# Sharing the adds of an attention layer between TensorE and VectorE: one gathered chunk of four on TensorE, or two

## The chip, the cores and the metric

The kernel runs as one program on one core of a Trainium2 chip. The metric is the device time of one execution in microseconds (us), from the first to the last instruction. Three executions of the kernel before took 1926.28, 1930.35 and 1936.67 us; their median, 1930.35 us, is the time before. About half a per cent (some 10 us) is what a measurement of this kernel can tell from no change: the three runs lie 0.5% apart.

The engines are named as in the profile: PE is TensorE (matmuls; PEld is its weight loads), DVE is VectorE, ACT is ScalarE, POOL is GpSimd, SP is the engine that issues most plain DMAs. "Granted clock" is the share of its full clock that TensorE is allowed at a time.

## The reference

The program is a graph network of four layers on 2708 nodes with 128 features, each followed by a residual add and a layer norm. Only the last layer, layer 3, is touched. For each of four heads it computes, with x the nodes' features and A the (sparse) adjacency matrix,

```
x1 = x @ w1
x2 = x @ w2
E  = leaky_relu(x1[:, None, :] + x2[None, :, :], negative_slope=0.01)
s  = E @ a
s  = tanh(s / 8.0) * 8.0
s  = exp(s) * A
s  = s / sum(s, axis=-1)
out = leaky_relu(s @ x @ Wlin.T, negative_slope=0.01)
```

and then joins the heads with one more matrix `w`. So every edge (i, j) needs, for each head, 128 sums x1[i] + x2[j], a leaky relu of each, and the dot product of the result with the head's vector `a`. The kernel writes leaky_relu(z) as 0.01 z + 0.99 max(z, 0). The first part is linear and is kept as four ready numbers per node; what is left per edge is max(z, 0) times 0.99 a, summed over 128 features, for four heads: 512 products and four sums.

## The kernel before, in words

The adjacency matrix has about 0.6% of its entries set, so the kernel lists each node's edges and works on edges. Nodes are sorted by degree and laid out in 24 blocks (`BLOCKS3`, lines 47 to 51). A block is cut into *steps* (`quads`, line 1527): 100 in all; fifteen of the 24 blocks have four or five. One step handles four *chunks*, and a chunk is up to 128 edges, one edge to a partition.

For a step `i` the loop at line 1541 does this:

- POOL gathers, one indirect DMA per chunk (`fetch`, line 1530; `gather`, line 246), one row per edge from a table in DRAM: 512 numbers of x2 (four heads of 128), 128 of x, and four linear terms. The row lands in `g4[:, r, :]`, r from 0 to 3. Nine such buffers (`GOT`) stand ready, so POOL runs up to eight steps ahead.
- PE puts x1 of each edge's own node into PSUM (`repeated`, line 1350): for chunk r a matmul whose weights are rows 32r to 32r+31 of a table of zeros and ones, so the four chunks use four different strips of the array. Chunks 0 to 2 go to three banks of the tile `z3`, chunk 3 to the tile `z1`. A further matmul, with the 128x128 identity as weights, adds chunk 3's gathered x2 onto `z1` (line 1363). Both tiles have one buffer, so the matmuls for step i+1 wait until step i has been read.
- DVE adds `z3` to the gathered x2 of chunks 0 to 2 (line 1555), in place in `g4`. Then it finishes chunk 3 with four instructions, one per head, that take max(z, 0) * 0.99a and the sum over 128 features at once (`scores`, line 1373). Then the products of the other chunks (`products`, line 1381), in place: three chunks in an even step (56 of the 100), two in an odd step (44).
- ACT sums the products, one instruction per chunk and head, with the sum falling out beside a dummy output (`sums_of_products`, line 1389): 12 in an even step, 8 in an odd one. In an odd step DVE does chunk 2 with four more instructions of line 1373.

Between these, `step()` (line 1514) lets three queues of unfinished work advance by one piece each, three times in a loop pass: `closing` (`rest`, line 1394: after each pair of steps, the linear terms, tanh and exp, the softmax sum by a small matmul at line 1414, its reciprocal at 1419, the weights `wm` at 1422, and eight matmuls at line 1435 that weigh and add the gathered x); `finishing` (`finish`, line 1443: once per block, a copy of that result, matmuls with Wlin at 1456, leaky relu by 1461 on ACT and 1463 on DVE, matmuls with w at 1469 and 1475); and `preparing` (`own_terms`, line 1311: x1 of the next block by the matmuls 1316, 1323 and 1324, the copies 1319 and 1327 on ACT, and line 1330 on DVE).

The program holds the order of each of PE, DVE and ACT as it is written (`manual_schedule`, line 1249); each works its list strictly in that order. On PE, the matmuls of `repeated` for step i+1 stand behind the first `step()` of step i and ahead of its products.

Of the kernel before, what the change touches and what calls it, by code (L numbers as in the profile page):

```python
# [9 lines left out]
FP = mybir.dt.float32  # L10
AF = mybir.ActivationFunctionType
ALU = mybir.AluOpType
# [3 lines left out]
P = 128  # L16
# [13 lines left out]
HD = HEADS * D  # L30
# [55 lines left out]
def gnn_resnorm_kernel(  # L86
# [21 lines left out]
    nc = tc.nc  # L108

    const = ctx.enter_context(tc.tile_pool(name="const", bufs=1))  # L110
    ident = const.tile([P, P], FP, name="ident")
# [225 lines left out]
    with ExitStack() as layer:  # L337
# [316 lines left out]
        for g in KINDS:  # L654
            j = 32 // g
# [198 lines left out]
        def own_row(b):  # L854
            n = BLOCKS[b][1]
            x_s = mine.tile([P, 2, D], FP, name="x_s", bufs=3)
            nc.sync.dma_start(
                x_s[0:n],
                dx_dram[int(b >= SPLIT)][b * P : b * P + n, 0 : 2 * D].rearrange(
                    "p (t d) -> p t d", t=2  # L860
                ),
            )
            return x_s
# [169 lines left out]
        ahead = own_row(0)  # L1033
        left = list(range(SPLIT, NBLK))
        for i, b in enumerate(TURNS):
            if i == SPLIT - 2:
                sorted_lists(1)
            x_s, ahead = ahead, own_row(TURNS[i + 1]) if i + 1 < NBLK else None
# [7 lines left out]
            for _ in range(2 if i < 1 else 1):  # L1046
                if left:
                    e = left.pop(0)
# [15 lines left out]
            for _ in range(2 if i in (9, 10, 11) else 1):  # L1064
                if i and again:
                    e = again.pop(0)
# [31 lines left out]
    with ExitStack() as layer:  # L1098
# [26 lines left out]
        for b0, count, n in quads():  # L1125
            a = accs2[b0 // 4].rearrange("p (j d) -> p j d", d=D)[0:n, b0 % 4 : b0 % 4 + count]
            h = hb[0:n, b0 : b0 + count]
# [3 lines left out]
            for j in range(count):  # L1131
                nc.tensor.matmul(
                    ps_v[:, 0:D], lhsT=ones[0:n, :], rhs=sq[0:n, j, :],
                    start=(b0 + j == 0), stop=(b0 + j == NBLK - 1),
# [48 lines left out]
        for b0, count, n in quads():  # L1183
            h = hb[0:n, b0 : b0 + count]
# [54 lines left out]
    with ExitStack() as layer:  # L1239
# [4 lines left out]
        ps_z = layer.enter_context(tc.tile_pool(name="s3_ps_z", bufs=1, space=PSUM))  # L1244
# [18 lines left out]
        a_99 = work.tile([P, HEADS, D], FP, name="a_99")  # L1263
        nc.vector.tensor_scalar(a_99, a_all, 0.99, None, ALU.mult)
        a_ps = ps_a.tile([P, HD], FP, name="a_ps")
# [84 lines left out]
        def repeated(b, j, g4):  # L1350

            g, _ = BLOCKS3[b]
            e = g * (P // g)
            z3 = ps_z.tile([P, 3, HD], FP, name="z3")
            z1 = ps_z.tile([P, HD], FP, name="z1")
            for r in range(4):
                rows = slice(32 * r, 32 * r + 32)
                nc.tensor.matmul(  # L1358
                    z3[0:e, r, :] if r < 3 else z1[0:e],
                    lhsT=copies[g][rows, j, :], rhs=own[b][1][rows, :],  # L1360
                    start=True, stop=r < 3, skip_group_check=r == 3,
                )
            nc.tensor.matmul(  # L1363
                z1[0:e], lhsT=ident[0:e, 0:e], rhs=g4[0:e, 3, 0:HD],
                start=False, stop=True, skip_group_check=True,
            )
            return z3, z1

        def scores(e, r, z, a, g4, sc):

            for hd in range(HEADS):
                part_of = slice(hd * D, (hd + 1) * D)
                nc.vector.scalar_tensor_tensor(  # L1373
                    g4[0:e, r, part_of], z[0:e, part_of], 0.0, a[0:e, part_of],
                    ALU.max, ALU.mult, accum_out=sc[0:e, hd : hd + 1],
                )

        def products(e, g4, count):

            z = g4[0:e, 0:count, 0:HD]  # L1380
            nc.vector.scalar_tensor_tensor(  # L1381
                z, z, 0.0, a_ps[0:e].unsqueeze(1).to_broadcast((e, count, HD)), ALU.max, ALU.mult
            )

        def sums_of_products(e, g4, sc, count):
            for r in range(count):
                for hd in range(HEADS):
                    junk = small.tile([P, D], BF, name="sum_junk")
                    nc.scalar.activation(  # L1389
                        junk[0:e], g4[0:e, r, hd * D : (hd + 1) * D], AF.Identity,  # L1390
                        accum_out=sc[0:e, r, hd : hd + 1],
                    )
# [121 lines left out]
        def step(early=True):  # L1514
            for queue, most in ((finishing, 1), (closing, 2), (preparing, 1)):
                if queue is not preparing or early:
                    for work_of in list(queue[:most]):
                        if next(work_of, "done") == "done":
                            queue.remove(work_of)

        def prepare(b):
            own[b] = (own_rows(b),)
            yield from own_terms(b)
# [4 lines left out]
        gathered = {}  # L1528

        def fetch(i):  # L1530
            b, j = quads[i]
            e = BLOCKS3[b][0] * (P // BLOCKS3[b][0])
            g4 = got.tile([P, 4, RW], FP, name="g4")
            for r in range(4):
                ch = CHUNK3[b] + 4 * j + r
                gather(g4[0:e, r, :], t2_dram, idx3[0:e, ch : ch + 1])
            gathered[i] = g4

        fetch(0)
        ahead = repeated(*quads[0], gathered[0])  # L1540
        for i, (b, j) in enumerate(quads):
            g, jj = BLOCKS3[b]
            e = g * (P // g)
            if j == 0:
                if b + 1 < NB3:
                    preparing.append(prepare(b + 1))
            if j % 2 == 0:
                sc, g4s = small.tile([P, 8, HEADS], FP, name="sc_s", bufs=4), []
            g4, (z3, z1) = gathered.pop(i), ahead
            g4s.append(g4)  # L1550
            sc4 = sc[:, 4 * (j % 2) : 4 * (j % 2) + 4, :]
            if i + 1 < len(quads):
                fetch(i + 1)
            z = g4[0:e, 0:3, 0:HD]
            nc.vector.tensor_tensor(z, z, z3[0:e], ALU.add)  # L1555
            scores(e, 3, z1, a_99.rearrange("p h d -> p (h d)"), g4, sc4[:, 3, :])
            step()
            if i + 1 < len(quads):
                while quads[i + 1][0] not in own or len(own[quads[i + 1][0]]) < 3:
                    step()  # L1560
                ahead = repeated(*quads[i + 1], gathered[i + 1])
            count = 2 if j % 2 else 3
            products(e, g4, count)
            step()
            sums_of_products(e, g4, sc4, count)
            if count == 2:
                scores(e, 2, g4[:, 2, 0:HD], a_ps, g4, sc4[:, 2, :])
            step()
            if j % 2 or j == jj - 1:
                closing.append(rest(b, list(range(j - j % 2, j + 1)), g4s, sc))  # L1570
# [526 lines left out]
```

## Time and profile before

| what | value |
|---|---|
| median of three runs | 1930.35 us |
| profiled execution, its own time | 1936.67 us |
| its span, first to last instruction | 1936.7 us |
| layer 3's loop, from the first matmul of line 1358 to the last gathered step's work | 1122 to 1905 us, 783 us |
| PE busy, share of the whole span, granted clock | 64%, 0.667 of full |
| DVE, ACT, POOL busy, share of the whole span | 60%, 40%, 46% |

The profiled execution is the slowest of the three, 0.3% above the median, and its span is the whole of its time. Shares over the whole span average four layers with different limits; what matters here is the loop of layer 3, two fifths of the time. The chain of waits that the page gives ends in the output's write and does not reach back into the loop, so the loop has to be read from its waits, groups, timeline and windows.

### The profile page before, as it was taken

The numbers are of one execution on the slowest core, as the hardware profiler recorded it, in microseconds if no ns is written. First come the engines' busy times: TensorE is split into PE (matmuls) and PEld (weight loads), VectorE is DVE, ScalarE is ACT, GpSimd is POOL, SyncE is SP. The second block draws the span as 40 slices with busy tenths as digits, with TensorE's granted clock in tenths as the row PEclk, the third lists the DMA queues.
The fourth block names the chain that finished last, engine by engine and source line by source line (L and its number), as shares of the span: only waits on it lengthen the run. The fifth ranks groups of instructions, "written<-read, shape, count | busy, mean of one in ns | idle before, by whom it ended". The sixth has DMA issues, their size and how long they took to land. (4 is left out here: it accounts for less than half of the span.)

```text
span 1936.7 us, 23643 instructions
## 1 busy us (share of the span) xinstructions
PE 1240.9 (64%) x5771; PEld 864.1 (45%) x5771; DVE 1166.6 (60%) x4895; ACT 776.5 (40%) x3156; POOL 892.8 (46%) x1003
## 2 busy tenths in 40 slices
PE   7974313353446553554673748888788788878885
PEld 7973212242334442554663314544444444444444
DVE  8997445675635423433447417777678677676774
ACT  3565345543324210211122415555455555445553
POOL 1004654445653366445331474655555556555430
PEclk9986555555555576776676756676676777666675
DMA  8642645666545525223231574865566655756540
GB/s 283 238 150 79 131 140 165 174 183 174 141 103 142 177 43 160 95 92 140 79 113 44 167 239 131 212 190 163 145 196 183 182 166 160 191 150 192 150 115 7
DMA packets 167676, 289.63 MB, mean 150 GB/s; under 512 B 49600, under 2 KB 121502, under 8 KB 160429
## 3 DMA queue, kind: packets, MB, share of 16 engines
q0 software_dynamic: 60496, 190.77, 34.4%
q1 hardware_dynamic: 99489, 92.57, 15.6%
q10 hardware_dynamic: 7544, 4.69, 1.0%
q8 instruction: 48, 0.79, 0.2%
q14 instruction: 99, 0.81, 0.1%
HBM read 242.51 MB, written 45.36 MB: 149 GB/s over the span
## 5 line engine op out<-in xcount | busy, mean ns | idle before, releaser
L247 POOL DMA_INDIRECT g<-t_dram,idx x400 | 398.6, 996 | 316.0 <-issue 178.9
L247 POOL DMA_INDIRECT msg<-d_dram,idx x368 | 348.6, 947 | 260.2 <-issue 164.8
L1389 ACT ACTIVATE sum_junk<-g 126x128 bf16<-126x128 f32 (+3 forms) x1024 | 301.3, 296 | 142.4 <-issue 59.8
L1358 PE MATMUL z<-x,copies 32*126 32x512 f32 (+3 forms) x800 | 221.3, 944 | 65.8 <-DVE g L1555 45.0
L969 PE MATMUL pt_a<-ident,rows 128*128 128x128 f32 (+2 forms) x475 | 114.1, 395 | 144.4 <-ACT at_sb L974 79.5
L1555 DVE TENSOR_TENSOR g<-g,z 126x1536 f32<-126x1536 f32 (+3 forms) x100 | 175.0, 1750 | 44.0 <-DMA g<-t_dram,idx 15.3
L1018 PE MATMUL acc<-x_nat,at_rows 128*128 128x128 f32 (+2 forms) x968 | 160.7, 326 | 52.3 <-DMA at_rows<-at_dram,perm 26.5
L1389 ACT ACTIVATION_READ_ACCUMULATOR sum_junk<-g 126x1 f32 (+3 forms) x1024 | 191.6, 187 | 0.0
L1018 PEld LDWEIGHTS acc<-x_nat,at_rows 128*128 128x128 f32 (+2 forms) x968 | 144.1, 232 | 65.5 <-issue 38.7
L1363 PE MATMUL z<-g,ident 126*126 126x512 f32 (+3 forms) x200 | 169.3, 941 | 0.7 <-issue 0.7
L1435 PE MATMUL po_s<-wm,g 126*128 126x24 f32 (+6 forms) x800 | 128.6, 316 | 58.5 <-DVE wm L1422 56.2
L1435 PEld LDWEIGHTS po_s<-wm,g 126*128 126x128 f32 (+3 forms) x800 | 124.8, 243 | 75.6 <-DVE wm L1422 67.9
L969 PEld LDWEIGHTS pt_a<-ident,rows 128*128 128x128 f32 (+2 forms) x475 | 82.9, 205 | 167.5 <-ACT at_sb L974 92.8
L884 DVE SCALAR_TENSOR_TENSOR own<-msg,ls,own 128x128 f32<-128x128 f32 (+1 forms) x302 | 105.6, 350 | 85.4 <-ACT msg L899 28.5
L1381 DVE SCALAR_TENSOR_TENSOR g<-g,a_ps 126x1536 f32<-126x1536 f32 (+6 forms) x100 | 151.0, 1510 | 0.0
L420 PE MATMUL acc<-x_nat,rows 128*128 128x129 f32 (+3 forms) x1012 | 128.5, 288 | 26.0 <-DMA rows<-in_adj_dram 14.9
L420 PEld LDWEIGHTS acc<-x_nat,rows 128*128 128x128 f32 (+2 forms) x1012 | 123.0, 198 | 31.2 <-DMA rows<-in_adj_dram 16.0
L1358 PEld LDWEIGHTS z<-x,copies 32*126 32x126 f32 (+3 forms) x800 | 67.8, 261 | 100.3 <-issue 46.5
L899 ACT ACTIVATE msg<-msg 128x896 f32<-128x896 f32 (+4 forms) x55 | 50.4, 917 | 132.9 <-DVE msg L896 92.1
L1373 DVE SCALAR_TENSOR_TENSOR g<-z,a 126x128 f32<-126x128 f32 (+3 forms) x400 | 91.9, 285 | 19.5 <-remote 9.2
L445 DVE FIND_INDEX8 ci<-cv,rows 128x8 uint32<-128x247 f32 (+2 forms) x242 | 98.7, 408 | 0.0
L1363 PEld LDWEIGHTS z<-g,ident 126*126 126x126 f32 (+3 forms) x200 | 42.0, 263 | 124.3 <-issue 117.3
(302 smaller groups left out, 2132.2 us busy)
## 6 DMA issues: line engine op xcount, KB each, us to landing
rows<-in_adj_dram SPq DMA_DIRECT2D x34, 1354.0 KB
at_dram<-at_sb SPq DMA_DIRECT2D x105, 256.0 KB
g<-t_dram,idx POOLq DMA_INDIRECT x400
msg<-d_dram,idx POOLq DMA_INDIRECT x368
t_dram<-t_row SPq DMA_DIRECT2D x21, 256.0 KB
x_s<-dx_dram SPq DMA_DIRECT2D x21, 128.0 KB
at_dram<-at_sb SPq DMA_DIRECT2D x21, 64.0 KB
t_dram<-x_nat SPq DMA_DIRECT2D x5, 256.0 KB
```

The costliest lines, as they stand in the source:

```text
L247: nc.gpsimd.indirect_dma_start(out=dst, out_offset=None, in_=table[0:N, :], in_offset=bass.IndirectOffsetOnAxis(ap=index, axis=0),)
L420: nc.tensor.matmul(accs0[k][0:m, c0 : c0 + f1 - f0], lhsT=rows[0:n, j0 : j0 + m], rhs=x_nat[0:n, b, f0:f1], start=k not in started, stop=( ...
L445: nc.vector.max_index(out=ci[0:n, at], in_max=cv[0:n, at], in_values=rows[0:n, c0 : c0 + cw])
L884: nc.vector.scalar_tensor_tensor(to, m, v, last, ALU.mult, ALU.add)
L969: nc.tensor.transpose(pt[0:m, j, 0:n], rows[0:n, c0 : c0 + m], ident[0:n, 0:n])
L1018: nc.tensor.matmul(accs2[ib // 4][0:m, (ib % 4) * D : (ib % 4 + 1) * D], lhsT=at[0:n, i0 : i0 + m], rhs=xw[0:n, b, :], start=(k == 0 and i ...
L1358: nc.tensor.matmul(z3[0:e, r, :] if r < 3 else z1[0:e], lhsT=copies[g][rows, j, :], rhs=own[b][1][rows, :], start=True, stop=r < 3, skip_g ...
L1363: nc.tensor.matmul(z1[0:e], lhsT=ident[0:e, 0:e], rhs=g4[0:e, 3, 0:HD], start=False, stop=True, skip_group_check=True,)
L1381: nc.vector.scalar_tensor_tensor(z, z, 0.0, a_ps[0:e].unsqueeze(1).to_broadcast((e, count, HD)), ALU.max, ALU.mult)
L1389: nc.scalar.activation(junk[0:e], g4[0:e, r, hd * D : (hd + 1) * D], AF.Identity, accum_out=sc[0:e, r, hd : hd + 1],)
L1435: nc.tensor.matmul(po[:, p0 * HEADS : (p0 + g) * HEADS], lhsT=g4s[i][0:e, r, HD : HD + D], rhs=wm[0:e, 4 * i + r, :, :], start=True, stop= ...
L1555: nc.vector.tensor_tensor(z, z, z3[0:e], ALU.add)
```

## The change

`repeated` now leaves x1 of chunks 0 and 1 in a two-bank tile `z2` and gives chunks 2 and 3 a tile of one bank each (`z1_2`, `z1_3`, together `zs`); it adds the gathered x2 to both by the identity. PSUM use stays at four banks. DVE adds only chunks 0 and 1. Chunk 2's products become one DVE instruction that reads `zs[0]` in PSUM and writes over the gathered x2. `products` always handles two chunks. ACT sums chunks 2, 0 and 1, in that order, in every step, and DVE's four extra instructions in odd steps are gone.

```diff
-            z3 = ps_z.tile([P, 3, HD], FP, name="z3")
-            z1 = ps_z.tile([P, HD], FP, name="z1")
+            z2 = ps_z.tile([P, 2, HD], FP, name="z2")
+            zs = [ps_z.tile([P, HD], FP, name=f"z1_{r}") for r in (2, 3)]
             for r in range(4):
                 rows = slice(32 * r, 32 * r + 32)
                 nc.tensor.matmul(
-                    z3[0:e, r, :] if r < 3 else z1[0:e],
+                    z2[0:e, r, :] if r < 2 else zs[r - 2][0:e],
                     lhsT=copies[g][rows, j, :], rhs=own[b][1][rows, :],
...
-            nc.tensor.matmul(
-                z1[0:e], lhsT=ident[0:e, 0:e], rhs=g4[0:e, 3, 0:HD],
-                start=False, stop=True, skip_group_check=True,
-            )
-            return z3, z1
+            for r in (2, 3):
+                nc.tensor.matmul(
+                    zs[r - 2][0:e], lhsT=ident[0:e, 0:e], rhs=g4[0:e, r, 0:HD],
+                    start=False, stop=True, skip_group_check=True,
+                )
+            return z2, zs
...
-        def products(e, g4, count):
+        def products(e, g4):
 
-            z = g4[0:e, 0:count, 0:HD]
+            z = g4[0:e, 0:2, 0:HD]
...
-        def sums_of_products(e, g4, sc, count):
-            for r in range(count):
+        def sums_of_products(e, g4, sc, chunks):
+            for r in chunks:
...
-            z = g4[0:e, 0:3, 0:HD]
-            nc.vector.tensor_tensor(z, z, z3[0:e], ALU.add)
-            scores(e, 3, z1, a_99.rearrange("p h d -> p (h d)"), g4, sc4[:, 3, :])
+            z, a_row = g4[0:e, 0:2, 0:HD], a_99.rearrange("p h d -> p (h d)")
+            nc.vector.tensor_tensor(z, z, z2[0:e], ALU.add)
+            nc.vector.scalar_tensor_tensor(
+                g4[0:e, 2, 0:HD], zs[0][0:e], 0.0, a_row[0:e], ALU.max, ALU.mult
+            )
+            scores(e, 3, zs[1], a_row, g4, sc4[:, 3, :])
             step()
...
-            count = 2 if j % 2 else 3
-            products(e, g4, count)
+            products(e, g4)
             step()
-            sums_of_products(e, g4, sc4, count)
-            if count == 2:
-                scores(e, 2, g4[:, 2, 0:HD], a_ps, g4, sc4[:, 2, :])
+            sums_of_products(e, g4, sc4, (2, 0, 1))
             step()
```

No DMA, no step of the three queues and no order among them changes.

More of the change, by code (lines that the diff above doesn't have):

```diff
@@ L1358, in repeated @@
                 nc.tensor.matmul(
-                    z3[0:e, r, :] if r < 3 else z1[0:e],
+                    z2[0:e, r, :] if r < 2 else zs[r - 2][0:e],
                     lhsT=copies[g][rows, j, :], rhs=own[b][1][rows, :],
-                    start=True, stop=r < 3, skip_group_check=r == 3,
+                    start=True, stop=r < 2, skip_group_check=r >= 2,
                 )
-            nc.tensor.matmul(
-                z1[0:e], lhsT=ident[0:e, 0:e], rhs=g4[0:e, 3, 0:HD],
-                start=False, stop=True, skip_group_check=True,
-            )
-            return z3, z1
+            for r in (2, 3):
[4 more added lines that the diff above has]
+            return z2, zs
         def scores(e, r, z, a, g4, sc):
@@ L1376, in scores @@
                 )
-        def products(e, g4, count):
-            z = g4[0:e, 0:count, 0:HD]
+        def products(e, g4):
+            z = g4[0:e, 0:2, 0:HD]
             nc.vector.scalar_tensor_tensor(
-                z, z, 0.0, a_ps[0:e].unsqueeze(1).to_broadcast((e, count, HD)), ALU.max, ALU.mult
+                z, z, 0.0, a_ps[0:e].unsqueeze(1).to_broadcast((e, 2, HD)), ALU.max, ALU.mult
             )
-        def sums_of_products(e, g4, sc, count):
-            for r in range(count):
+        def sums_of_products(e, g4, sc, chunks):
+            for r in chunks:
                 for hd in range(HEADS):
@@ L1548, in gnn_resnorm_kernel @@
                 sc, g4s = small.tile([P, 8, HEADS], FP, name="sc_s", bufs=4), []
-            g4, (z3, z1) = gathered.pop(i), ahead
+            g4, (z2, zs) = gathered.pop(i), ahead
             g4s.append(g4)
```

## The prediction

> **What bounds the kernel now.** The change touches the loop of layer 3 alone, so I read that stretch, not the page's shares. First the windows: how busy each engine is there, and at which granted clock.
>
> ```profile
> core 0: us, PE busy (x) PEld busy (x) DVE busy (x) ACT busy (x) POOL busy (x), PEclk, DMA share, GB/s
> 1121.80:1905.00 783.20, 632.67 (x2455) 356.87 (x2455) 541.89 (x1855) 397.16 (x2367) 414.96 (x417) 0.68 0.60 169
> ```
>
> No engine is full. PE (81%) and DVE (69%) take turns, and PE runs at 0.68 of its clock. The waits in the loop after its start (1125 to 1905 us) say who waits for whom:
>
> ```profile
> DVE al L1330 <- PE few_ps L1414: 32.2, 13, 4.0
> DVE inv L1419 <- PE few_ps L1475: 30.8, 14, 4.8
> ...
> DVE g L1373 <- PE z L1363: 5.0, 15, 0.4
> ```
>
> ```profile
> PE po_s L1435 <- DVE wm L1422: 55.3, 28, 6.8
> PE z L1358 <- DVE g L1555: 45.0, 29, 7.8
> ```
>
> DVE waits for PE at the ends of PE's list (after 1414 and 1475, which stand behind the identity matmul of the next step), and hardly for the identity itself (5 us). PE waits for DVE's add and for the weights `wm`. So it is a loop of dependences that crosses from one to the other. Then the groups by shape, for prices:
>
> ```profile
> L1555 DVE TENSOR_TENSOR g<-g,z 126x1536 f32<-126x1536 f32 x52 | 91.0, 1750 | 18.4 <-DMA g<-t_dram,idx 6.6 <-remote 5.4 <-PE po_s L1435 3.6
> ...
> L1381 DVE SCALAR_TENSOR_TENSOR g<-g,a_ps 126x1536 f32<-126x1536 f32 x30 | 52.4, 1746 | 0.0
> ...
> L1381 DVE SCALAR_TENSOR_TENSOR g<-g,a_ps 126x1024 f32<-126x1024 f32 x22 | 26.6, 1209 | 0.0
> ...
> L1463 DVE SCALAR_TENSOR_TENSOR lin_s<-pl_s,lin_s 128x512 f32<-128x512 f32 x6 | 4.2, 692 | 8.6 <-ACT lin_s L1461 5.8 <-issue 2.8
> ```
>
> And the timeline of PE, for the same matmul at two clocks (start, duration):
>
> ```profile
> 1440.26 2.07 PE L1363 MATMUL z<-g,ident 126*126 126x512 f32 x2
> 1442.13 1.89 PE L1456 MATMUL pl_s<-o_ts,wlin_s 128*128 128x112 f32 x8
> ...
> 1445.91 1.12 PE L1363 MATMUL z<-g,ident 128*128 128x512 f32 x2
> 1446.87 0.38 PE L1469 MATMUL few_ps<-own_x,pick 128*112 128x128 f32 x2
> ```
>
> From its start to the next matmul's, the identity costs 1.87 us at half clock and 0.96 at full. Last, windows of 3.4 us, for the matmuls that touch `z` alone, in order (after the length their PE, PEld and DVE time; third from the end is the granted clock):
>
> ```profile
> 1445.77:1449.18 3.41, 1.27 (x6) 0.30 (x2) 0.00 (x0) 1.00 0.76 236
> 1449.18:1452.59 3.41, 0.00 (x0) 0.00 (x0) 1.57 (x1) 0.96 0.06 16
> 1452.59:1456.01 3.42, 3.09 (x9) 1.32 (x10) 1.34 (x10) 0.50 0.53 124
> 1456.01:1459.42 3.41, 1.79 (x2) 0.22 (x2) 2.36 (x9) 0.54 0.89 280
> 1459.42:1462.84 3.42, 2.20 (x10) 0.61 (x10) 0.00 (x0) 1.00 0.83 267
> 1462.84:1466.25 3.41, 0.90 (x6) 0.31 (x6) 2.60 (x9) 0.96 0.43 115
> 1466.25:1469.66 3.41, 3.41 (x7) 1.00 (x4) 1.44 (x1) 0.50 0.79 230
> ```
>
> The clock is granted in such pieces, full or half. A full-clock piece poor in `z` matmuls (0.00, 0.90) is followed by half clock, a rich one (1.27) by another full one; half clock ends after pieces packed with them. So the clock follows how much the wide matmuls run, and this change adds wide matmuls.
>
> **The change part by part.** Prices are start-to-start, some 0.08 us under the durations on DVE.
>
> *DVE.* The add shrinks from 1.67 us to 1.13 (the 1024 row of line 1381; at 1536 the two forms agree). New is one 512-wide instruction out of PSUM, 0.62 us by the 692 ns row. An even step's products go from 1.67 to 1.13; an odd step loses four line-1373 instructions at 0.21. Even: -0.54+0.62-0.54 = -0.46 us, 56 times; odd: -0.54+0.62-0.84 = -0.76, 44 times. Sum -59 us of DVE.
>
> *ACT.* 4 sums more in 44 steps, 0.295 us each by their spacing in the timeline: +52 us. Chunk 2's sums are ready before the products and run beside them, since ACT is half idle (397 of 783 us). Their cover is DVE's next add, new instruction and scores, 2.6 us, against 2.4 us of the other eight sums: 0.2 us is left. If that is gone the price is at most 1.18 us in each odd step, 52 us.
>
> *PE.* One identity pair more per step: +96 us at full clock, +187 at half, 139 at the loop's 0.69 (0.96/0.69 each). Chunk 2's matmul of `repeated` now waits for the new DVE instruction and chunk 3's for the scores; while they wait, the queue behind them stands (identities, then block work of 1456, 1323, 1414). The first two chunks start 0.54 us sooner than now.
>
> *POOL and SP* issue the same DMAs. POOL's 400 gathers at 1.30 us are 5.2 us per step, of 7.8 now: cover enough.
>
> What of this lies on the path I walk through a block of four steps, from one `wm` to the second next and so on, each engine's list in order, with full-clock prices (four strips 1.05, identity 0.96, sixteen records of line 1435 1.75, line 1475's work 1.1) and then half-clock ones (1.95, 1.87, 3.4, 2.2).
>
> - Full clock, steps one and two now: DVE 4.69 (add 1.67, scores 0.85, lines 1400/1403 0.4, products 1.67, 1409 0.1), then add and scores to 7.2; line 1330 waits for ACT, whose 12 sums start at 4.6 and whose copy 1327 ends at 8.75; then 0.15, products 1.13, `wm` 0.9, four scores 0.84: 11.75. With the change the sums start at 3.8 and the copy ends at 7.9; to `wm` 10.15.
> - Steps three and four now: the path goes from the scores (7.2) through PE (strips, identity, 1469/1475) to 10.4, then 1.75 of DVE: 12.2. Then: 6.8, strips 1.05, two identities, 1.1, `wm` 0.9: 12.0.
> - So 23.95 becomes 22.15 at full clock. At half clock PE's list is nearly unbroken and all four new identities lie on it: 33.35 becomes 39.7 (+4 x 1.87, less 1.1 of DVE).
>
> Two undisturbed blocks measured: 1423.17 to 1450.97 and on to 1477.96, 27.4 us each. Between 23.95 and 33.35 that is 37% of the work at half clock. At the same share the changed block takes 22.15 + 0.37 x 17.55 = 28.6 us, 1.2 more; the two are equal at a share of 30%.
>
> Does the share stay? In the full-clock walk the stretches without `z` matmuls are two per block now, 3.9 us (ahead of each line 1435) and 4.8; then 2.0 and 4.1. Only the second is longer than a piece of clock, so I expect one fall per block instead of two; and at half clock the packed run per step is 5.7 us instead of 3.9, which ends the spell sooner. A spell of two pieces falling in steps one and two costs 14.55-10.15 = 4.4 us there. With one spell in seven blocks of ten a block takes 25.2 us; with stalls, short blocks and first steps broken as now I allow shares from 16% to 26%: 25.0 to 26.7 us. That is -2.4 to -0.7 per block, times 24.5 blocks (98 steps): -59 to -17 us, and I take -36, just under the middle, since some spells will begin in steps three and four, where they cost more.
>
> [...] The windows above show falls with PE far from idle, so the sum goes by them.
>
> The profiled execution took 1936.7 us, span and own time alike, 6.3 above the median 1930.35. So 1936.7-36 = 1900.7 for such an execution, 1894 for the median.
>
> **The rivals.**
> - *The clock doesn't rise* (the slower side). Place: the second half of each block, where at half clock z, two identities, 1456, z, two identities, 1475 stand in one line. It decides from a half-clock share above 30%. At 37%: +1.2 x 24.5 = +30, 1960; at 50%: 30.9 us, +86, 2016. For it: PE is 81% busy and heads the waits; against it: the windows.
> - *ACT takes the gain.* The 0.2 us of slack goes and lines 1400/1405 start late in most odd steps: about 30 of the 52 us back, 1924. For it: DVE already waits 4.3 us for those sums at 1400; against it: ACT is idle half the time.
> - *The clock stays full nearly throughout*: 22.2 to 24 us a block, -83 to -127 us; with the pauses of 5 to 8 us in which all engines stand (1649.6 to 1655.2 for one, and not of this change's making), 1803 to 1847; I name 1835, since each pause will still cost a spell.
> - *No change in what runs* is excluded: both program orders differ in every step.
>
> **How the numbers follow.** Forecast 0.48, clock not rising 0.30, ACT 0.14, full clock 0.08. A measurement tells about 0.5% (10 us). Faster is the forecast and the full clock: 0.56; same is the ACT case: 0.14; slower 0.30. The likeliest case's own range is 1871 to 1913. The range reaches up into the no-rise case past its 37% value to a share near 42% (1980) and down to the full-clock case (1840).
>
> **What would show it.** Granted clock in the loop from 0.68 to about 0.8; line 1363's successor with 400 records; the add near 1.2 us, the new instruction near 0.69, all products near 1.21; `wm` waits of PE (55 us) smaller; line 1330's wait smaller. It is wrong if the clock stays below 0.72, if DVE's wait at the scores for the identity grows from 5 us to tens, or if lines 1400/1405 wait for the sums.

## The result and the profile after

The changed kernel takes 1936.07 us in the median of 20 runs, the kernel before 1930.24 in 20 runs: ratio 1.0041, 95% interval 1.0024 to 1.0058. The forecast of 1894 is missed by 42 us, and the sign is the other one, if barely. The profiled execution took 1931.8 us (span 1930.1), 4 us under its median. The profile before lies 6 us above its own, so some 10 us of a difference between the two profiles is scatter.

Nearly every term of work came out as forecast. The loop of layer 3 after the change, in the same window as before, same columns:

```profile
core 0: us, PE busy (x) PEld busy (x) DVE busy (x) ACT busy (x) POOL busy (x), PEclk, DMA share, GB/s
1121.80:1905.00 783.20, 655.23 (x2671) 355.81 (x2671) 487.17 (x1611) 448.25 (x2727) 414.18 (x415) 0.81 0.59 168
```

VectorE (DVE) lost 54.7 us of work (541.9 to 487.2; forecast 59), ScalarE (ACT) gained 51.1 (397.2 to 448.3; forecast 52), the granted clock rose from 0.68 to 0.81 (forecast "about 0.8"), and PE's busy time grew by 23 us only, since the faster clock paid for most of the hundred new identity matmuls. The prices by shape are the forecast's too (1.2, 1.2 and 0.69 us):

```profile
L1556 DVE TENSOR_TENSOR g<-g,z 126x1024 f32<-126x1024 f32 x52 | 63.2, 1215 | 9.5 <-PE z L1358 5.3 <-PE pl_s L1457 2.2 <-issue 1.0
...
L1382 DVE SCALAR_TENSOR_TENSOR g<-g,a_ps 126x1024 f32<-126x1024 f32 x52 | 63.0, 1211 | 0.0
...
L1557 DVE SCALAR_TENSOR_TENSOR g<-z,a 126x512 f32<-126x512 f32 x52 | 35.7, 687 | 27.5 <-remote 10.4 <-issue 4.5 <-PE po_s L1436 3.7
```

Still the loop is nearly as long as it was (766.0 us in place of 770.5, from the first add to the last). The waits after its start (1125 to 1905 us), in the order that matters here: total, times, longest.

```profile
PE po_s L1436 <- DVE wm L1423: 48.4, 22, 7.8
ACT sum_junk L1390 <- ACT sum_junk L1390: 46.8, 69, 1.3
...
DVE inv L1420 <- PE few_ps L1476: 36.0, 15, 4.7
...
DVE inv L1420 <- remote: 29.2, 6, 8.6
...
PE z L1358 <- DVE g L1557: 19.0, 3, 13.5
...
DVE g L1557 <- PE z L1364: 11.4, 12, 1.5
...
PE z L1358 <- DVE g L1556: 8.3, 7, 3.4
...
DVE g L1374 <- PE z L1364: 8.0, 10, 1.0
DVE al L1330 <- PE few_ps L1415: 7.7, 6, 3.3
```

The forecast waits shrank: line 1330's from 32.2 to 7.7, `wm` from 55.3 to 48.4, and that of the strips of line 1358 for DVE's add from 45.0 to 8.3, or to 27.3 with the wait for the new instruction at line 1557 (19.0, of which one wait is 13.5). DVE waits for the identities 8.0 us at the scores and 11.4 at the new instruction, where it was 5.0 in all. What grew beside that is odd: ScalarE waits for itself, and line 1420 waits for a releaser that the trace cannot name ("remote"). Both were there before the change, and smaller:

```profile
DVE inv L1419 <- remote: 21.8, 4, 6.7
...
ACT sum_junk L1389 <- ACT sum_junk L1389: 17.2, 33, 1.2
```

Waits of 5 to 9 us stand among others of 1 us. Not one of these is the price of an instruction.

The timeline shows what such waits are. This is the end of a fourth step of a block (1408.5 to 1418.3 us), in which the granted clock was full: start, duration, instruction, and in brackets the idle time before it.

```profile
1414.24 0.31 ACT L1390 ACTIVATE sum_junk<-g 126x128 bf16<-126x128 f32 x1 [1.25 <-ACT sum_junk L1390]
1414.34 1.03 PE L1476 MATMUL few_ps<-wout_s,lin_s 128*112 128x128 f32 x8
...
1415.69 0.31 ACT L1390 ACTIVATE sum_junk<-g 126x128 bf16<-126x128 f32 x1 [0.65 <-ACT sum_junk L1390]
...
1417.10 0.31 ACT L1390 ACTIVATE sum_junk<-g 126x128 bf16<-126x128 f32 x1 [1.00 <-ACT sum_junk L1390]
1417.31 1.45 SPq L1294 DMA_DIRECT2D own_x<-x_dram  x4
...
1417.41 0.36 DVE L1420 RECIPROCAL inv<-few_ps 126x32 f32<-126x32 f32 x1 [2.85 <-remote]
```

PE's matmuls of line 1476 end at 1415.37; line 1420, which needs no more than their completion, starts at 1417.41, 2.04 us later. SyncE's line 1294, which waits for the matmul of line 1470 before them, starts 0.10 us earlier. ScalarE, whose sums wait for the completion of the sum three before (three `sum_junk` buffers), starts two of them at 1415.69 and 1417.10, with nothing else to do between. The trace's semaphore events say the same more exactly. Seven PE instructions that signal end between 1412.17 and 1415.38; PE's semaphore has no event in that time, and then seven of them between 1417.08 and 1417.38, most 0.04 us apart. Line 1294 starts 0.02 us after the sixth and line 1420 0.03 us after the seventh. So PE's completions were held, the first for 4.9 us, and then delivered in one burst. The step took 9.85 us; on another chip, below, the same step takes 7.85.

How often this happens can be counted: an event of an engine's semaphore counts as late when none of the engine's instructions that signal it has ended within 0.15 us before. In the loop 274 of PE's 640 events are late (43%), and 159 of ScalarE's 1060 (15%); before the change it was 166 of 452 (37%) and 143 of 929 (15%). Of DVE's 573 events none is late (11 of 541 before). Events are also missing from the trace (PE has 770 instructions that signal in the loop, DVE 887), and a missing event tells nothing of when its completion arrived; the shares are of the events that are there.

### The profile page after: what moved, and what is told of

It is laid out like the page before. It is cut to its first block, busy times and chain, and to the rows that moved or that the text cites. A ratio compares the mean times of both kernels' runs of the same rounds, so it can differ in the third digit from the quotient of the medians.

```text
span 1930.1 us, 24100 instructions
## 1 busy us (share of the span) xinstructions
PE 1260.2 (65%) x5971; PEld 859.7 (45%) x5971; DVE 1110.4 (58%) x4643; ACT 825.7 (43%) x3508; POOL 895.3 (46%) x1003
## 5 line engine op out<-in xcount | busy, mean ns | idle before, releaser
L1390 ACT ACTIVATE sum_junk<-g 126x128 bf16<-126x128 f32 (+3 forms) x1200 | 353.1, 296 | 78.4 <-ACT sum_junk L1390 46.8
L1364 PE MATMUL z<-g,ident 126*126 126x512 f32 (+3 forms) x400 | 251.3, 760 | 0.0
L1358 PE MATMUL z<-x,copies 32*126 32x512 f32 (+3 forms) x800 | 209.0, 765 | 48.2 <-DVE g L1557 19.0
L1390 ACT ACTIVATION_READ_ACCUMULATOR sum_junk<-g 126x1 f32 (+3 forms) x1200 | 225.3, 188 | 0.0
L1018 PE MATMUL acc<-x_nat,at_rows 128*128 128x128 f32 (+2 forms) x968 | 157.7, 324 | 50.8 <-issue 31.3
L1364 PEld LDWEIGHTS z<-g,ident 126*126 126x126 f32 (+3 forms) x400 | 83.0, 231 | 165.4 <-issue 160.2
L1436 PE MATMUL po_s<-wm,g 126*128 126x24 f32 (+6 forms) x800 | 114.8, 297 | 51.3 <-DVE wm L1423 49.3
L1556 DVE TENSOR_TENSOR g<-g,z 126x1024 f32<-126x1024 f32 (+3 forms) x100 | 121.5, 1215 | 34.0 <-remote 13.9
L1436 PEld LDWEIGHTS po_s<-wm,g 126*128 126x128 f32 (+3 forms) x800 | 111.7, 221 | 62.9 <-DVE wm L1423 54.0
L1382 DVE SCALAR_TENSOR_TENSOR g<-g,a_ps 126x1024 f32<-126x1024 f32 (+3 forms) x100 | 121.2, 1212 | 0.0
L1374 DVE SCALAR_TENSOR_TENSOR g<-z,a 126x128 f32<-126x128 f32 (+3 forms) x400 | 91.7, 285 | 27.4 <-issue 8.1
L1557 DVE SCALAR_TENSOR_TENSOR g<-z,a 126x512 f32<-126x512 f32 (+3 forms) x100 | 68.6, 686 | 54.0 <-remote 25.5
```

Source lines behind the costliest of these rows:

```text
L1018: nc.tensor.matmul(accs2[ib // 4][0:m, (ib % 4) * D : (ib % 4 + 1) * D], lhsT=at[0:n, i0 : i0 + m], rhs=xw[0:n, b, :], start=(k == 0 and i ...
L1358: nc.tensor.matmul(z2[0:e, r, :] if r < 2 else zs[r - 2][0:e], lhsT=copies[g][rows, j, :], rhs=own[b][1][rows, :], start=True, stop=r < 2, ...
L1364: nc.tensor.matmul(zs[r - 2][0:e], lhsT=ident[0:e, 0:e], rhs=g4[0:e, r, 0:HD], start=False, stop=True, skip_group_check=True,)
L1374: nc.vector.scalar_tensor_tensor(g4[0:e, r, part_of], z[0:e, part_of], 0.0, a[0:e, part_of], ALU.max, ALU.mult, accum_out=sc[0:e, hd : hd ...
L1382: nc.vector.scalar_tensor_tensor(z, z, 0.0, a_ps[0:e].unsqueeze(1).to_broadcast((e, 2, HD)), ALU.max, ALU.mult)
L1390: nc.scalar.activation(junk[0:e], g4[0:e, r, hd * D : (hd + 1) * D], AF.Identity, accum_out=sc[0:e, r, hd : hd + 1],)
```

## The experiments

Three theories: (1) the longer list of head sums on ScalarE took the gain; (2) the added identity's price on PE took it; (3) the late completions did, which come with the gathers. Four chips, called A to D here, ran the groups below; ratios are to the kernel before on the same chip, with 95% intervals. The changed kernel itself was measured only above and ran on none of these beside its variants, so where a ratio is held against its 1.0041, two measurements on what may be two chips are compared. Loop lengths are from the first add to the last.

**One part at a time (chip A, before 1915 us).** ScalarE's part alone:

```
-            count = 2 if j % 2 else 3
+            count = 3
```

> The kernel before, with the products of three chunks and their twelve head sums on ScalarE in every step (in 44 odd steps four VectorE instructions of line 1373 go, 0.84 us, the products grow by 0.54 us, and ScalarE gets four sums more, 52 us in all); PE as before. It is the ScalarE part of the change alone. Theory 1: slower by 15 to 40 us, lines 1400 and 1403 start late after odd steps. Theory 2: faster by up to 13 us. Theory 3: within 10 us of 1930, ScalarE's waits for its own sums grow from 17 to about 45 us as in the changed kernel.

Measured: 1.0025 (0.9994 to 1.0056), ScalarE busy 441 us in place of 391, its self-waits 16.2 us past the eighth step, as before the change. So 50 us more of ScalarE's work costs at most 0.6%. Theory 3 had these self-waits grow to about 45 us, and they did not: the longer list alone doesn't make them. The other way round, the changed kernel with ScalarE as before:

```
+            if j % 2:
+                scores(e, 2, zs[0], a_row, g4, sc4[:, 2, :])
+            else:
-            nc.vector.scalar_tensor_tensor(g4[0:e, 2, 0:HD], zs[0][0:e], ...)
+                nc.vector.scalar_tensor_tensor(g4[0:e, 2, 0:HD], zs[0][0:e], ...)
...
-            sums_of_products(e, g4, sc4, (2, 0, 1))
+            sums_of_products(e, g4, sc4, (0, 1) if j % 2 else (2, 0, 1))
```

> The changed kernel, but in odd steps chunk 2 is scored by four VectorE instructions straight from its bank in place of line 1557, and ScalarE sums two chunks there, as before the change: PE as changed, ScalarE as before, VectorE +0.22 us in each of 44 odd steps. Theory 1: the gain comes back, about 1905. Theory 2: 1936 to 1946. Theory 3: 1930 to 1946.

Measured: 1.0032 (1.0015 to 1.005). The gain does not come back, and theory 1 falls; ScalarE's self-waits, 18.2 us past the eighth step, went without the time going. Its last form, that the self-waits cost the time:

```
-                    junk = small.tile([P, D], BF, name="sum_junk")
+                    junk = small.tile([P, D], BF, name="sum_junk", bufs=16)
```

> The changed kernel with 16 buffers of `sum_junk` in place of 3, so that a head sum no longer waits for the completion of the sum three before it. ScalarE's waits for itself (47 us in the loop, 17 before the change) should go. Theory 1, if it is these waits: 1905 to 1915. Theory 2: 1936. Theory 3: the waits go, but VectorE and PE still get completions late, 1920 to 1936.

Measured: 0.9994 (0.9975 to 1.0013), self-waits past the eighth step 12.6 us, where the changed kernel's profile has 46.1. That is 0.5% under the changed kernel's 1.0041 and 0.4% under the run before it on the same chip: a small part, as theory 3 has it.

PE's part alone was meant to be a second identity in the kernel before:

```
             for r in range(4):
+                if r == 3:
+                    nc.tensor.matmul(z1[0:e], lhsT=ident[0:e, 0:e], rhs=g4[0:e, 2, 0:HD], start=True, stop=True)
```

> The kernel before, with one more identity matmul per step on TensorE alone (it writes chunk 2 into `z1`, and chunk 3's strip then starts that bank afresh, so nothing of the result changes); VectorE and ScalarE keep their work. It is the PE part of the change alone. Theory 1 (the head sums of ScalarE took the gain): PE's part is harmless, the clock in the loop rises from 0.67 to about 0.8 and the time is 1900 to 1930. Theory 2 (the identity's price itself took the gain): the 0.96 us per step at full clock stays on the path in half of the steps, time 1960 to 1990. Theory 3 (the odd steps are set by completions that arrive late while the gathers of a pair run, whatever the engines' speed): clock up to about 0.8 and time within 10 us of 1930.

Measured: 1.0747 (1.0719 to 1.0776), far over every expectation, because the edit does more than was meant. The four strips of line 1358 (32 rows each, two records each) run side by side when they follow each other: in the timeline of the kernel before, eight records take 1.14 us at full clock.

```profile
1459.69 1.14 PE L1358 MATMUL z<-x,copies 32*128 32x512 f32 x8
```

Put between the third and the fourth strip, the new matmul splits them. PE's timeline in that kernel, at the clock's fall from full to half:

```profile
1504.99 1.13 PE L1362 MATMUL z<-x,copies 32*128 32x512 f32 x6 [0.48 <-DVE g L1559]
1506.05 1.80 PE L1358 MATMUL z<-g,ident 128*128 128x512 f32 x2
1507.78 2.07 PE L1362 MATMUL z<-x,copies 32*128 32x512 f32 x2
1509.78 2.08 PE L1367 MATMUL z<-g,ident 128*128 128x512 f32 x2
```

The fourth strip alone (2.07 us) costs as much as an identity (2.08), so the edit added two matmuls' time per step, not one: PE's busy time in the loop went from 623 to 800 us, and the clock to 0.73 only. It says nothing on the price of one identity. The three strips ahead of the split took 1.13 us, as long as all four together in the kernel before (1.14).

**The identity taken out of the changed kernel (chip B, before 1931 us).** The tuple `with_x2` is `(3,)` in every step; for the second run it is `(2, 3) if j % 4 < 2 else (3,)`, so that only the second half of each block goes without (43 of the 100 steps; the expectation counts 47):

```
+            with_x2 = (3,)
...
-            for r in (2, 3):
+            for r in with_x2:
```

> The changed kernel without the identity matmul of chunk 2 (line 1557 reads the bank after its strip alone, so x2 of one chunk in four is left out of the result). VectorE and ScalarE keep the work of the changed kernel, PE that of the kernel before. Theory 2 (the added identity, 100 of them, is what took the gain): at least 60 us under the changed kernel, 1860 or less where that takes 1923 on this chip. Theory 3 (late completions during the gathers set the odd steps): within 15 us of the changed kernel, and the granted clock in the loop falls back towards 0.68.

> The same, but the identity of chunk 2 is left out only in the steps with j%4 of 2 and 3, the second half of a block, where the forecast's walk had the path run through PE (12.2 us before, 12.0 after). Theory 2, with the price in the second half: most of what leaving out all of them gives, in 47 of 100 steps. Theory 2, with the price spread evenly: half of it. Theory 3: within 10 us of the changed kernel.

Measured: 0.9989 (0.9961 to 1.0017) without any, and 1.0099 (1.0061 to 1.0138) without those of the second half. A hundred identities less give 10 us against the changed kernel's ratio; 43 of them less give nothing, and are 11 us slower if anything. The loop without them shows why:

```profile
1122.38:1882.58 760.20, 640.02 (x2423) 358.30 (x2423) 479.34 (x1586) 443.02 (x2678) 412.95 (x414) 0.68 0.61 173
```

PE is busy for 640 us with 199 matmul records less than the changed kernel has in the same stretch (2622, 643.7 us): the clock falls back to 0.68 and the remaining matmuls take longer. So the run takes away the identities and the faster clock together, and theory 2, which had 60 us for them, falls. And DVE's 57 us less than before, with PE's matmuls and clock as before, give next to nothing as well: VectorE's work does not hold the loop. PE's might, by this run alone, for its busy time is nearly the same in all three loops (623, 644 and 640 us); the next pair tells.

**Half of the gathers (chip B).** The same edit in both kernels, GpSimd and the DMAs alone:

```
+        held = [work.tile([P, 4, RW], FP, name=f"held{i}") for i in range(GOT)]
...
-            g4 = got.tile([P, 4, RW], FP, name="g4")
-            for r in range(4):
+            g4 = held[i % GOT]
+            for r in (0, 2):
```

> The kernel before with the gathers of chunks 0 and 2 alone (200 in place of 400, into nine tiles cleared once; chunks 1 and 3 work on what those tiles hold, so the result is another). It halves the bursts of gathers and leaves PE, VectorE and ScalarE their work. Theory 3: the odd steps shorten, 40 us or more off the loop. Theory 2: the loop is as long as before within 15 us.

> The changed kernel with the same halved gathers. Theory 3: with the bursts halved the forecast's gain appears, the loop 25 to 50 us shorter than that of the kernel before with halved gathers. Theory 2: no such gain, the two within 10 us.

Measured: before 0.9498 (0.9442 to 0.9555), 1829.2 us; changed 0.9313 (0.9269 to 0.9358), 1797.0 us. With half of the gathers the change is 32 us faster, 1.8% (four executions of each), where the forecast had 36. The loops, first the kernel before and then the changed one:

```profile
1136.30:1783.38 647.08, 582.79 (x2422) 326.74 (x2423) 532.63 (x1838) 385.79 (x2329) 215.32 (x216) 0.74 0.37 103
```

```profile
1137.42:1756.42 619.00, 577.08 (x2622) 321.64 (x2622) 476.29 (x1587) 433.81 (x2682) 217.00 (x217) 0.88 0.39 109
```

PE's matmuls are the same in number, its clock is higher, and the part of the loop in which it is idle falls from 147 to 64 us before the change and from 122 to 42 after it; so more than half of what went is time in which PE waited. The waits of the changed one past its eighth step: the long ones are gone, and so is "remote" at line 1420.

```profile
DVE inv L1420 <- PE few_ps L1476: 32.7, 20, 2.6
...
PE po_s L1436 <- DVE wm L1423: 23.1, 21, 1.2
...
ACT sum_junk L1390 <- ACT sum_junk L1390: 15.6, 25, 1.0
```

PE's late events fall to 24 of 707 (3%) in the kernel before and 85 of 778 (11%) in the changed one. Theory 3 stands on these chips: with fewer gathers the lateness goes, and the change gains.

**Bytes, number, or late rows (chip C, before 1933 us).** All 400 gathers with rows of 1288 bytes in place of 2576:

```
-                gather(g4[0:e, r, :], t2_dram, idx3[0:e, ch : ch + 1])
+                nc.gpsimd.indirect_dma_start(
+                    out=g4[0:e, r, 0 : RW // 2], out_offset=None,
+                    in_=t2_dram.rearrange("n (h w) -> (n h) w", h=2)[0:N, :], ...
```

> The changed kernel with all 400 gathers, each of rows half as long (1288 bytes in place of 2576, from a view of the same table; the other half of each tile keeps its cleared values, so the result is another). It keeps the number of gathers, rows and completions of the changed kernel and takes the bytes of the halved gathers. If the bytes in flight are what delays the loop (theory 3a), the time falls as with the halved gathers, to about 1800 (ratio 0.93 to 0.95). If the number of gathers or rows does it (3b), it stays near the changed kernel, ratio 0.99 to 1.0. If the loop waits for late rows or buffers (3c), in between, as the rows arrive sooner.

> The kernel before with the same short rows. 3a: about 1830 (ratio 0.95), and the changed kernel with short rows some 30 us under it, as with halved gathers. 3b: ratio about 1.0.

Measured: 1.0075 (1.0045 to 1.0104) and 0.9996 (0.9973 to 1.0019). The share of the DMA engines in the loop falls from 0.60 to 0.34, and the time does not. Past the eighth step the loop is shorter (before 694 to 657 us, changed 687 to 662), which a loop that starts 12 to 17 us later and slower first steps give back; halving the gathers took 100 and 119 us off the same stretch. PE's late events are 32% in the changed kernel with short rows. So it is mostly the number of gathers, not their bytes. Ten buffers in place of nine:

```
-GOT = 9
+GOT = 10
```

> The changed kernel with ten buffers of `g4` in place of nine, so a gather may run one step further ahead. 3a and 3b: no change, within 5 us of the changed kernel. 3c: faster by 10 us or more.

Measured: 1.0038 (1.0012 to 1.0064), the changed kernel again. A tenth buffer is worth nothing, so buffers are not what the loop waits for.

**Gathers spaced out (chip C).** A memset ahead of each gather, into columns that the gather fills:

```
+                nc.gpsimd.memset(g4[0:e, r, 0:256], 0.0)
                 gather(g4[0:e, r, :], t2_dram, idx3[0:e, ch : ch + 1])
```

> The changed kernel with a GpSimd memset of 256 columns ahead of each gather, into the columns that the gather then fills (the result is the same): some 0.3 to 0.45 us more between gathers, so the eight of a pair go out over 13 to 14 us in place of 10.4, and fewer bytes are in flight at a time. 3a: long waits shrink, 10 to 40 us faster than the changed kernel, ratio 0.98 to 0.997. 3b: unchanged, ratio about 1.004. 3c: rows and buffers come later, slower, ratio 1.01 or more.

Measured: 0.9651 (0.9622 to 0.9681), 1867.4 us, 66 us under the kernel before on that chip, and more than any of the three expectations has. GpSimd's order puts two memsets ahead of two gathers, so a pair of steps' eight gathers go out over some 12 us. The loop:

```profile
1122.36:1824.03 701.67, 624.92 (x2622) 345.64 (x2623) 484.94 (x1587) 436.48 (x2680) 529.92 (x809) 0.83 0.67 188
```

Against the changed kernel's profile GpSimd is busier by 116 us and the loop 64 us shorter, at the same clock and the same work on the other engines. So how the gathers come sets the loop here, while nobody has less to do. It is not plain lateness that went: ScalarE's late events fall from 15 to 3%, but PE's are still 38%, and line 1420's waits for "remote" past the eighth step are 37.9 us, not 29.2. Which part of the gain is which was not shown.

**The fourth chip (D, before 1608 us).** These were meant to tell the spacing from the memset's wait, and to see what the kernel before gains:

> The kernel before with the GpSimd memset of 256 columns ahead of each gather. If it is the gathers' density that holds both kernels, this one is faster too, by 30 to 60 us (ratio 0.97 to 0.985), and the changed kernel with the same memsets (ratio 0.965) stands 10 to 35 us under it: the forecast's gain, freed. If the memsets suit only the changed kernel, the ratio here is 0.99 to 1.01.

> The changed kernel with a memset of 8 columns in place of 256 ahead of each gather: the same instructions and waits, a third of the added time. If the spacing does it, little of the gain is left, ratio 0.985 to 1.004. If it is the memset's wait or the place that it gives the gathers in GpSimd's order, the ratio is again about 0.965.

> 512 columns: the gathers of a pair take about 16 us, more than the 15 us of a pair of steps. If the density sets the time, the long waits shrink further, but GpSimd becomes the bound, 16 us times 49 pairs, about 785 us of loop, ratio 0.98 to 1.02.

> The changed kernel with the memsets of 256 columns and 16 buffers of `sum_junk`: the two edits that each took time off it. If late completions of ScalarE's own sums still cost something with the gathers spaced, 3 to 10 us less than with the memsets alone; otherwise the same, ratio about 0.965.

Measured: 1.0074 (1.0053 to 1.0096), 0.9708 (0.9673 to 0.9742), 1.0522 (1.0489 to 1.0555) and 1.0063 (1.004 to 1.0085). Chip D runs the kernel before in 1608 us where A, B and C take 1915 to 1933, so the question put could not be answered there, but another was. Instructions take as long there (the 1024-wide add 1.21 us), and some 210 of the 325 us lie ahead of layer 3, whose loop starts at 912 us in place of 1122. The trace of the changed kernel with the small memsets has a completion event for nearly every instruction (765 for PE's 770), and none on the three engines is late by the count above; nor is any in the kernel before with memsets of 256 columns. The same step end as above, in the same block:

```profile
1131.40 1.04 PE L1476 MATMUL few_ps<-wout_s,lin_s 128*112 128x128 f32 x8
...
1131.60 1.35 SPq L1294 DMA_DIRECT2D own_x<-x_dram  x4
...
1132.48 0.36 DVE L1420 RECIPROCAL inv<-few_ps 126x32 f32<-126x32 f32 x1 [1.78 <-PE few_ps L1476]
```

From the end of line 1476 to line 1420 it is 0.04 us, where it was 2.04. The step takes 7.85 us. The loop, at twice the DMA share of the halved gathers, and its waits past the eighth step:

```profile
912.26:1518.40 606.14, 570.87 (x2622) 318.57 (x2622) 476.52 (x1586) 431.07 (x2677) 435.72 (x799) 0.88 0.81 218
```

```profile
DVE inv L1420 <- PE few_ps L1476: 37.6, 21, 3.1
...
PE po_s L1436 <- DVE wm L1423: 23.5, 22, 1.2
```

So on a chip without late completions the changed kernel with 400 tiny memsets is 46 us faster than the kernel before without them; that the memsets themselves are worth nothing there is likely, as the larger ones cost time, but the kernel before was not run with the tiny ones. The larger memsets cost there: with 512 columns PE waits 68.6 us for rows. With 256 columns on both sides the change gains nothing (1620.4 us before it, 1618.7 after it with 16 `sum_junk` buffers); GpSimd, busy for 529 of some 660 us of loop in both, is then the likely pace. A second time, on the same chip:

> Again the kernel before with memsets of 256 columns. The chip of the first time ran the kernel before in 1608 us in place of 1915 to 1933, without late completions, and there spacing cost 0.7%. On a chip with late completions (before at 1900 or more) I expect ratio 0.97 to 0.985, against 0.965 for the changed kernel with the same memsets; on one without them 1.005 to 1.01 again.

> Again the changed kernel with memsets of 8 columns, the nearest to the changed kernel itself: on a chip without late completions 0.971 again. On a chip with them: ratio 0.985 to 1.004 if it was the spacing in time that gave 0.965 with 256 columns, about 0.965 if it was the wait and the order.

Measured: 1.0102 (1.007 to 1.0134) and 0.9749 (0.9717 to 0.9782).

The mean step of the ten blocks that have four steps, from the starts of the add in each timeline (us), with the length of the block:

| kernel, chip | step 1 | 2 | 3 | 4 | block |
|---|---|---|---|---|---|
| before | 6.16 | 8.08 | 6.38 | 11.07 | 31.7 |
| after | 6.20 | 8.05 | 5.56 | 11.49 | 31.3 |
| before, half the gathers, B | 5.84 | 7.44 | 5.03 | 8.80 | 27.1 |
| after, half the gathers, B | 5.92 | 6.41 | 4.81 | 8.37 | 25.5 |
| after, memsets of 8, D | 5.84 | 6.84 | 4.51 | 7.89 | 25.1 |

The fourth steps on chip D lie within 7.84 and 8.00 us, all ten; in the changed kernel of the first profile they run from 7.87 to 16.45. The mean of the kernel before hides two kinds of block: five of the ten take 27.0 to 28.0 us and five 32.6 to 39.5. After the change the five shortest take 27.6 to 29.6, so even the quick blocks did not get shorter.

## Why the prediction was wrong

- **What bounds the loop.** "A loop of dependences that crosses from one to the other" was right as far as it went. The forecast read the waits at lines 1330 and 1419 as PE's list being long. Part of them was a completion on its way: the lines with "remote" and ScalarE's waits for itself were in the trace of before (21.8 us at line 1419, and 17.2), and were passed over.
- **VectorE and ScalarE**: right, within 5 us.
- **The clock**: right by its mean, 0.81, and in its direction. The reason given was fewer falls, one in seven blocks of ten, which would be 17 spells at half clock; 32 begin in the loop (43 before), and 23 on chip D. So the closeness of the mean is in part luck.
- **PE**: priced at 139 us more of work at the loop's clock; measured 23 us more of busy time, since the clock rose with it. Taking the identity out again, and the faster clock with it, gave 10 us.
- **The block walk**: right for a loop without the lateness. 25.2 us was forecast with one spell of half clock in seven blocks of ten, 25.0 to 26.7 allowed; 25.1, 24.7 (the second time) and 25.5 were measured where completions come on time or the gathers are halved. Steps three and four, "12.0" at full clock, took 12.4 on chip D; the terms listed for them add up to 11.8.
- **The step that failed is the sum over the blocks**: "Two undisturbed blocks measured", 27.4 us each (two of the five quick ones), and what a block gains "times 24.5 blocks", with the stalls "as now". 27.4 is the block of an undisturbed loop (27.1 with half the gathers), but the mean block of the profile was 31.7. The 4.6 us between them were taken as a constant that stays. They did not stay: with the changed kernel the difference is 5.8 (31.3 less 25.5). The mean block fell by 0.4 us where the forecast's 36 us need 1.5. Of the 1.6 us that a block gains undisturbed, 1.2 went there. The most of it is in step 4 (2.3 us over the undisturbed step before, 3.1 after) and step 2 (0.6 and 1.6). (These differences set the first two profiles against those of chip B.) Why the shorter loop loses more to late completions was not shown. The changed kernel has more of them to deliver, 770 signals of PE in the loop in place of 572, and 274 late events in place of 166; whether that is the reason no run tests.
- **The rivals.** "The clock doesn't rise" is refuted by 0.81. "ACT takes the gain" came nearest to the measured time (1924), for a reason that two runs refute. A case for "the time is held by something that none of the changed work touches" was missing, and the profile's mean block against the undisturbed one, 31.7 against 27.4, was the number that called for it.

Left open: on chip D the changed kernel was run only with memsets, and its gain there stands on the tiny ones being worth nothing; how much of the 66 us of spacing the kernel before would gain on A to C, and whether time or order gives them, was not measured; and what makes completions late on three chips and not on the fourth, with as many gathers, is unknown.

## What to carry to other kernels

When a loop's walk gives less than the mean of the profile, the rest is a term of its own: find the waits that no instruction's length explains (an engine that waits for itself, a releaser that cannot be named, the same row with a mean of 2 us and a longest of 8) before taking work off engines. Test such a term by halving what might cause it in both kernels, and compare the two changes, not the two times. And a change that is worth nothing on one chip may (here in its nearest version) be worth 2.5 to 3% on another, so a ratio belongs to the chip that it was measured on.

## What the runs showed of the hardware

- Completions can reach waiting engines late and in bursts: in the step shown, seven of PE's are delivered within 0.3 us, the first of them 4.9 us after its matmul's end, while gathers are issued one per 1.28 us. Halving the gathers cuts PE's late events from 37 to 3% in the kernel before and from 43 to 11% in the changed one, halving their bytes only to 32% in the changed one, and on chip D none was late at a DMA share of 0.81. The trace also lacks semaphore events in the first profiles (640 for 770 signals of PE, 573 for 887 of DVE) and hardly any on D (765 for 770). Whether the recording of the trace has a part in this, no run here shows.
- Taking matmuls away can leave PE as busy as it was: 640.0 us without the hundred identities at a clock of 0.68 (chip B), 643.7 with them at 0.82 (the profile after).
- The clock can fall without a long pause of PE. On chip D PE was busy for 571 of the loop's 606 us, its longest pause in the records was 3.4 us, the next 2.0, and the granted clock was 0.88, with 23 spells at half clock that begin in the loop. In the kernel before, 43 such spells begin in the loop; in two of the forecast's windows at whose ends the clock fell (1449.18 to 1452.59 and 1462.84 to 1466.25 us), all matmuls together, not those on `z` alone, kept PE busy for 2.16 and 2.23 of the 3.41 us.
- Four quarter-height strips took 1.14 us together at full clock, and three 1.13; split off behind another matmul, the fourth took 2.07 us at half clock, as much as a full-height one (2.08).
